# Two vision layers on one core: the step size moved into an exponential's bias, skips added to a diagonal, and shorter stage openings

## The chip, the cores and the metric

The kernel runs on one core of a Trainium2 chip. The metric is the device time of one execution in microseconds (us); lower is better. Five engines work side by side and are ordered only by semaphores: PE multiplies matrices (PEld is its loading of weights), DVE, ACT and POOL work elementwise, and SP issues the DMAs. Each engine takes its own instructions strictly in the order in which the program lists them.

## The reference

Two layers follow each other on 8 images of 64x64 tokens with 192 channels. Layer 0 is a state-space layer with 12 heads (two scan directions of 6 heads), a gate and an MLP. What matters of it:

```
dt = softplus(dt + dt_bias);  da = exp(dt * A);  dtx = dt[..., None] * xh
h = da_t * h + dtx_t * B_t;   y_t = sum_n h * C_t          # step by step over 4096 tokens
y = ys + Ds * xh
out = x + (y0 + y1) * silu(z) @ W_out;   out + W2(silu(W1 out + b1)) + b2
```

Layer 1 splits the channels: one half goes through three convolutions with batch norms, the other through a layer norm, a depthwise convolution and a selective scan in four directions with 192 channels and 16 states each; both halves are joined and the input added.

## The kernel before

**The main loop.** `selective_scan` computes the scan of layer 1. It runs over 3072 units, 384 per image. A unit is 8 channels with 16 states (128 partitions) and 1024 tokens. For each, SP fetches the step sizes (`fetch`, L1430), ACT makes the decays (`decay`, L1435, two units ahead), PE spreads the inputs (`spread`, L1443, one unit ahead), DVE weights them (L1458) and scans (L1465), POOL multiplies by C (L1467), ACT handles the last column (L1473, L1474), PE gathers four units at a time (L1485), ACT copies the result out of PSUM (y, L1490) and SP stores it. Every 16 units a tile is prepared (`prepare`, L1387 to L1430).

**Side stages.** While image b is scanned, the other work of later images runs beside it: for image b+1 `conv0`, `ssd` (layer 0's scan), `mlp0`, then for image b-1 `conv_branch` (with `scan_sums` aside) and `scan_outputs`, then `scan_inputs` and `transposed` for image b+1. Image 0 has its stages ahead of the loop, one after the other, and the last image's outputs come after it.

**Pacing.** Each unit has two halves, and in each `Beside.half` lets the current stage run on. Stages are generators: a number they yield is a cost that is taken from a credit, and the half ends when the credit is gone; an empty yield (`None`) ends the half at once, to let something land. `pause(n)` yields n of them. `spread_over` sets the credit per half so that the stages fill the image:

```
work = sum(self.costs.get(gen.__name__, 40.0) for gen in self.stages)
self.rate = own / halves + work / (halves - 13 * len(self.stages))
```

The costs are what the stages yielded for image 0 (190 and 78 for the branch and the outputs). Ahead of the loop, empty yields are passed over. `in_turn` interleaves the steps of one stage for successive items; `among` puts calls between the yields of a generator. All instructions are pinned to program order.

**The chunk scan.** `ssd` works through an image in 32 chunks of 128 tokens (for each direction two runs of 64 tokens). In each turn come `store`, `outputs`, `weigh`, `decays` and `fetch`, of successive chunks. `fetch` makes R on POOL (L594). `decays` loads X (L602, L605), transposes B and C (ps_t, copied by ACT to bc), and computes the exponents of the decays between all pairs of tokens for 6 heads x 64 columns in ps_d (L618, L619), from which ACT makes M by one exponential for each direction (L621, L624). `weigh` computes ps_g = B^T C (L634), scales the states (Hm, POOL, L637) and the inputs (xw, POOL, L639), multiplies M by ps_g (DVE, L643) and X by dt (dtx, POOL, L645). `outputs` adds to the states (ps_s, L655; Hm, DVE, L661; Hn, POOL, L663, and DVE, L677), multiplies them by C (ps_h, L671; yo, DVE, L681) and adds the pairs (ps_y): for each direction and head, M times dtx (L686), and for direction 0 also a diagonal `skip0` times X (L692), which holds Ds of both directions. `group` prepares dt and its running sums for 8 chunks at once (L533 to L577).

PSUM tiles outside the unit's own dB come from `cx.one`, which hands out four banks in rotation (eight ahead of the loop, while a second pool is open). A bank is free again when its last reader is done, so PE can wait for ACT or DVE to read what stood there.

Of the kernel before, what the change touches and what calls it, by code (L numbers as in the profile page):

```python
# [17 lines left out]
L = HH * WW  # L18
# [11 lines left out]
S = 64  # L30
# [79 lines left out]
def setup(cx, cp, dp, p0, p1):  # L110
# [105 lines left out]
    for n, v in (("eps", 1e-5), ("one", 1.0), ("minus", -1.0)):  # L216
        k[n] = cp.tile([128, 1], F32, tag=n, name=n)
        nc.gpsimd.memset(k[n], v)
# [77 lines left out]
def among(gen, calls):  # L296

    calls = list(calls)
    for n, cost in enumerate(gen):
        yield cost  # L300
        if n % 2 == 1 and calls:
            calls.pop(0)()
    for call in calls:
        call()
        yield None
# [72 lines left out]
def conv0(cx, x):  # L378
# [3 lines left out]
    with cx.pool("cw0") as wp, cx.pool("v0", 2) as vp:  # L382
# [98 lines left out]
        for j in range(NJ):  # L481
            pin(nc.sync.dma_start(out=diag[:, j], in_=k["diag0"][:, j]))
            yield None
        xp = wp.tile([128, 2 * NJ, 2 * NP0], F32, tag="xp0", name="xp0")
        for i in range(2):
            pin(nc.sync.dma_start(
                out=xp[64 * i : 64 * (i + 1)], in_=k["p0_xp"].rearrange("(j p) k m -> p j (k m)", p=64)
            ))
# [3 lines left out]
        yield from pause(2)  # L492
        load(1)
        yield from pause(2)
        load(1)
        for j in range(NJ):
            yield from project(0, j)
# [13 lines left out]
def ssd(cx):  # L511

# [14 lines left out]
    with cx.pool("g0", 2) as gp, cx.pool("s0", 2) as sp:  # L527
# [5 lines left out]
        def group(g):  # L533
# [19 lines left out]
            pin(nc.scalar.activation(dt, dt, AF.Softplus))  # L553
            cx.exp_again()
# [22 lines left out]
            groups[g] = both, over, *(t.rearrange(by_chunk, k=K2) for t in (dt, da, upto, toend))  # L577

        coming = group(0)
        for n in (8, 2, 2, 3, 2):  # L580
# [17 lines left out]
        def decays(c):  # L598
# [15 lines left out]
            M = sp.tile([128, 2, NH, S], F32, tag="M", name="M")  # L614
            R = st[c].pop("R")
            for d in range(2):
# [3 lines left out]
                if d == 1:  # L620
                    pin(nc.scalar.activation(flat(M[:, 0]), ahead, AF.Exp))  # L621
                yield 1.0
                ahead = ps
            pin(nc.scalar.activation(flat(M[:, 1]), ahead, AF.Exp))  # L624
            st[c].update(X=X, bc=bc, M=M)

        def weigh(c):

            _, over, dt, _, _, toend = groups[c // GC]
# [8 lines left out]
            xw = sp.tile([128, 2, NH, HP], F32, tag="xw", name="xw", bufs=1)  # L638
# [5 lines left out]
            dtx = sp.tile([128, 2, NH, HP], F32, tag="dtx", name="dtx", bufs=1)  # L644
            pin(nc.gpsimd.tensor_mul(dtx.rearrange(heads), X.rearrange(heads), bcast(dt[:, c % GC, :], 2, HP)))  # L645
            st[c].update(dtx=dtx, xw=xw, Hm=Hm)

        def outputs(c):

            both, over, _, _, upto, _ = groups[c // GC]  # L650
            X, bc, M, xw, dtx, Hm = (st[c].pop(v) for v in ("X", "bc", "M", "xw", "dtx", "Hm"))
# [1072 lines left out]
```

## Time and profile before

| | |
|---|---|
| median of 3 runs | 16537.61 us (16530.31 to 16537.72) |
| profiled execution | 16556.29 us, its span 16554.4 us |
| mean granted PE clock | 0.831 of full |
| DMA | 196 GB/s on average |
| first scan unit starts / last one starts | 913.1 us / 16290.4 us |

In the lines below, "L1465 DVE ... h<-dA,carry,dB 128x1024" is the instruction of line 1465 on DVE, the tiles that it writes and reads and their size, then how often it comes, its busy time in total, the mean duration of one in ns, and the idle time of the engine ahead of it with what ended that. A busy time counts overlapped instructions once, and a mean duration can overlap that of its neighbour. A window's line has its start and end, its length, and the busy time of each engine with the number of instructions.

### The profile page before, as it was taken

Reading aid. Unit: us, or ns where it says so; the run is one execution under the profiler, and the core shown is the slowest. Engines: PE = TensorE matmul, PEld = TensorE weight load, DVE = VectorE, ACT = ScalarE, POOL = GpSimd, SP = SyncE. Lnnn points to the kernel's source line nnn. Section 1 sums busy time; section 2 is a strip of 40 time slices with the busy share of each in tenths; the row PEclk is TensorE's granted clock in tenths of the full one; section 3 lists DMA queues with packets and bytes.
Section 4 is the critical chain, followed back from the end, with each engine's and each line's share of the span. In section 5 each row is a group of like instructions: output and inputs, shape, how many; then the busy total and the mean of one; then the engine's idle time right before and its main releaser. Section 6 shows DMA issues by size and latency. Waiting matters only on the chain.

```text
span 16554.4 us, 220424 instructions
## 1 busy us (share of the span) xinstructions
PE 13560.5 (82%) x75752; PEld 4803.7 (29%) x75752; DVE 12258.6 (74%) x9264; ACT 9901.5 (60%) x17354; POOL 10649.1 (64%) x5765
## 2 busy tenths in 40 slices
PE   8977887788977888888888789887898878878876
PEld 4423322332223321333213332233322333211111
DVE  2268888886778766887678876788767887778994
ACT  3365677565674656647566475665657556655653
POOL 3258766875568655686557865577655775566773
PEclk9987888889788896888878898788887889877766
DMA  3288878888787887888778878888778887788884
GB/s 90 84 218 198 214 196 227 194 209 202 182 226 192 202 208 184 222 193 207 205 195 208 199 199 207 206 202 198 196 195 212 200 209 203 193 224 201 214 209 125
DMA packets 1605044, 3248.22 MB, mean 196 GB/s; under 512 B 390536, under 2 KB 841752, under 8 KB 1603928
## 3 DMA queue, kind: packets, MB, share of 16 engines
q1 hardware_dynamic: 1603928, 3234.12, 78.5%
q8 instruction: 605, 9.91, 0.3%
q14 instruction: 511, 4.19, 0.1%
HBM read 2555.20 MB, written 678.18 MB: 195 GB/s over the span
## 4 chain that ended last, share of the span: by engine, by line
PE 41%; DMA 17%; DVE 16%; ACT 11%; POOL 8%; issue 5%; SPq 2%; DVEq 0%; POOLq 0%; ACTq 0%
DVE h L1465 9%; PE ps_cv L343 7%; DMA dA<-dld 5%; PE acc L1485 4%; DVE dB L1458 4%; PE ps_c L886 4%; POOL h L1467 3%; PE dB L1443 2%; ACT dA L1435 2%; PE ps_m L795 2%; PE ps_sum L1178 2%; PE ps_xp L1355 2%; DMA dus<-dud 2%; PE ps_y L686 1%; PE ps_var L1000 1%
## 5 line engine op out<-in xcount | busy, mean ns | idle before, releaser
L1467 POOL TENSOR_TENSOR h<-h,bc 128x1023 f32<-128x1023 f32 x3072 | 7229.2, 2354 | 4661.0 <-DVE h L1465 4123.4
L1465 DVE TENSOR_TENSOR_SCAN h<-dA,carry,dB 128x1024 f32<-128x1024 f32 x3072 | 7201.5, 2344 | 712.6 <-ACT dA L1435 224.1
L1458 DVE TENSOR_TENSOR dB<-dB,bc 128x1024 f32<-128x1024 f32 x3072 | 3742.3, 1218 | 1921.2 <-PE dB L1443 1909.4
L1435 ACT ACTIVATE dA<-dA,neg_a 128x1024 f32<-128x1024 f32 x3072 | 3505.9, 1141 | 44.2 <-DMA dA<-dld 39.1
L1485 PE MATMUL acc<-h,gather 128*32 128x512 f32 x12288 | 2310.3, 721 | 524.3 <-ACT h L1474 230.7
L1443 PE MATMUL dB<-dus,spread 24*128 24x512 bf16 x6144 | 1379.8, 434 | 849.4 <-DVE h L1465 764.0
L1490 ACT COPY y<-acc 128x512 f32<-128x512 f32 x1536 | 883.3, 575 | 944.0 <-PE acc L1485 818.5
L886 PE MATMUL ps_c<-p,conv_w 96*96 96x512 f32 x2304 | 1242.8, 668 | 70.2 <-ACT p L906 63.2
L1443 PEld LDWEIGHTS <-spread 24*128 24x128 bf16 x6144 | 309.6, 93 | 3099.6 <-issue 1452.3
L1473 ACT COPY carry<-h 128x1 f32<-128x1 f32 x3072 | 573.0, 187 | 947.5 <-DVE h L1465 944.4
L686 PE MATMUL ps_y<-dtx,M 64*64 64x64 f32 x12288 | 784.9, 258 | 333.6 <-DVE Hn L677 309.4
L1474 ACT ACTIVATE h<-h,bc 128x1 f32<-128x1 f32 x3072 | 905.2, 295 | 158.7 <-ACT carry L1473 3.0
L343 PE MATMUL ps_cv<-pad,diag 64*64 64x512 f32 x6912 | 835.6, 603 | 6.4 <-ACT y L1490 5.4
L686 PEld LDWEIGHTS ps_y<-dtx,M 64*64 64x64 f32 x12288 | 662.5, 169 | 492.7 <-issue 311.4
L1485 PEld LDWEIGHTS acc<-h,gather 128*32 128x32 f32 x12288 | 304.6, 117 | 1535.5 <-issue 938.2
L107 ACT ACT_TABLE_LOAD x577 | 740.3, 1283 | 10.2
L618 PE MATMUL ps_d<-R,after 128*128 128x384 f32 x1024 | 565.0, 642 | 72.5 <-POOL R L594 26.9
L613 ACT COPY bc<-ps_t 64x256 f32<-64x256 f32 x256 | 93.4, 365 | 855.9 <-PE ps_t L608 855.6
L886 PEld LDWEIGHTS ps_c<-p,conv_w 96*96 96x96 f32 x2304 | 368.5, 177 | 777.8 <-issue 686.8
L1355 PE MATMUL ps_xp<-u,xp 128*108 128x512 f32 x768 | 474.4, 706 | 98.9 <-DMA u<-u 86.1
L1394 POOL TENSOR_TENSOR du<-dl,u 128x1024 f32<-128x1024 f32 x192 | 452.2, 2355 | 127.0 <-ACT dl L1391 127.0
L373 PE MATMUL ps_h<-oa,w1a 128*128 128x256 f32 x1536 | 451.5, 414 | 58.6 <-ACT h L826 17.3
(243 smaller groups left out, 19239.9 us busy)
## 6 DMA issues: line engine op xcount, KB each, us to landing
dA<-dld SPq DMA_DIRECT2D x3072, 512.0 KB
dud<-terms SPq DMA_DIRECT2D x192, 768.0 KB
dus<-dud SPq DMA_DIRECT2D x2304, 64.0 KB
bc<-bcd SPq DMA_DIRECT2D x256, 512.0 KB
y<-yrows SPq DMA_DIRECT2D x256, 384.0 KB
u<-u SPq DMA_DIRECT2D x192, 512.0 KB
dld<-dl SPq DMA_DIRECT2D x192, 512.0 KB
y<-y SPq DMA_DIRECT2D x3072, 32.0 KB
```

What stands on the lines that cost most here:

```text
L343: pin(nc.tensor.matmul(ps[64 * b : 64 * (b + 1)].rearrange("p (h w) -> p h w", w=WW), lhsT=diag[:, t, :], rhs=pad[64 * i : 64 * (i + 1), b ...
L686: pin(nc.tensor.matmul(psy[d][here, h * HP : (h + 1) * HP], lhsT=M[here, d, h, :], rhs=dtx[here, d, h, :], start=True, stop=d == 1,))
L886: pin(nc.tensor.matmul(ps.rearrange("p (h w) -> p h w", w=WW), lhsT=w[:, t, :], rhs=pad[:, dy : dy + RB, dx : dx + WW], start=t == 0, stop ...
L1355: pin(nc.tensor.matmul(ps[:NXP], lhsT=k["xp"][:, g, t, :], rhs=u_of[m][t][:, here], start=t == 0, stop=t == 2))
L1435: pin(nc.scalar.activation(dAs[q], dAs[q], AF.Exp, scale=k["neg_a"][:, steps[m][1], t, i : i + 1]))
L1443: pin(nc.tensor.matmul(dBs[q][:, half, :], lhsT=k["spread"][at : at + 3 * UD, :], rhs=du_of[n][at : at + 3 * UD, i // 2, :], start=True, s ...
L1458: pin(nc.vector.tensor_mul(dBs[q], dBs[q], of(q)[0]))
L1465: pin(nc.vector.tensor_tensor_scan(order(h, g), order(dA, g), order(dB, g), carry, ALU.mult, ALU.add))
L1467: pin(nc.gpsimd.tensor_mul(h[:, rest], h[:, rest], C_[:, rest]))
L1474: pin(nc.scalar.activation(end, end, AF.Identity, scale=C_[:, last : last + 1]))
L1485: pin(nc.tensor.matmul(ps[32 * v : 32 * (v + 1)], lhsT=k["gather"], rhs=hs[q - 3 + v][:, here], start=True, stop=True))
L1490: pin(nc.scalar.copy(y[:, here], ps))
```

## The change

In `ssd`, the decays' exponent gets the logarithm of dt as a bias: exp(s + ln dt) = dt exp(s). The bias is a column for each head, so each of the two exponentials per chunk becomes six over 64 columns. Then M holds dt already, and dtx is not made; M is multiplied with X. `group` computes ln dt (with 1e-37 added) after softplus. The skips are added on POOL to direction 0's M, at the opening of `outputs`, and the skip matmuls are gone. xw gets two buffers. Yields of `outputs` fall from 1.7 and 1.1 to 1.1 and 1.1.

The openings of the stages are shortened: `conv0` loads its first diagonal alone and the others between the steps of the first projection (it had also loaded the second rows twice), `mlp0` begins its gate after three halves and loads the rest between its yields, `conv_branch` loads the second convolution's weights and `scan_inputs` its diagonals within the work; pauses in `ssd`, `transposed` and `scan_outputs` are shorter. `transposed` copies two parts between pauses, with four buffers. In `spread_over` 13 becomes 9.

```diff
-def among(gen, calls):
+def among(gen, calls, n=2):
...
-        if n % 2 == 1 and calls:
+        if i % n == n - 1 and calls:
             calls.pop(0)()
@@ conv0
-        for j in range(NJ):
+        def load_diag(j):
             pin(nc.sync.dma_start(out=diag[:, j], in_=k["diag0"][:, j]))
-            yield None
...
+        load_diag(0)
         yield from pause(2)
         for j in range(NJ):
             pin(nc.gpsimd.memset(pads[j], 0.0))
-        yield from pause(2)
+        yield from pause(1)
+        for j, calls in enumerate(([lambda: load_diag(1)], [lambda: load_diag(2)], [load_xp])):
+            yield from among(project(0, j), calls, 1)
         load(1)
-        yield from pause(2)
-        load(1)
-        for j in range(NJ):
-            yield from project(0, j)
@@ ssd, group
             pin(nc.scalar.activation(dt, dt, AF.Softplus))
+            ln_dt = gp.tile([128, GC * K2], F32, tag="ln_dt", name="ln_dt")
+            pin(nc.scalar.activation(ln_dt, dt, AF.Ln, bias=k["tiny"]))
             cx.exp_again()
@@ ssd
-        for n in (8, 2, 2, 3, 2):
+        for n in (7, 1, 1, 2, 1):
@@ ssd, decays
+            def exp(d, ps):
+                for h in range(NH):
+                    bias = groups[c // GC][2][:, c % GC, d * NH + h : d * NH + h + 1]
+                    pin(nc.scalar.activation(M[:, d, h, :], ps[:, h * S : (h + 1) * S], AF.Exp, bias=bias))
...
-                    pin(nc.scalar.activation(flat(M[:, 0]), ahead, AF.Exp))
+                    exp(0, ahead)
...
-            pin(nc.scalar.activation(flat(M[:, 1]), ahead, AF.Exp))
+            exp(1, ahead)
@@ ssd, weigh
-            xw = sp.tile([128, 2, NH, HP], F32, tag="xw", name="xw", bufs=1)
+            xw = sp.tile([128, 2, NH, HP], F32, tag="xw", name="xw")
...
-            dtx = sp.tile([128, 2, NH, HP], F32, tag="dtx", name="dtx", bufs=1)
-            pin(nc.gpsimd.tensor_mul(dtx.rearrange(heads), X.rearrange(heads), bcast(dt[:, c % GC, :], 2, HP)))
@@ ssd, outputs
+            pin(nc.gpsimd.tensor_add(M[:, 0], M[:, 0], k["skip0"]))
...
-                            psy[d][here, h * HP : (h + 1) * HP], lhsT=M[here, d, h, :], rhs=dtx[here, d, h, :],
-                            start=True, stop=d == 1,
+                            psy[d][here, h * HP : (h + 1) * HP], lhsT=M[here, d, h, :], rhs=X[here, d, h, :],
+                            start=True, stop=True,
                         ))
-                    if d == 0:
-                        for here in chunks:
-                            pin(nc.tensor.matmul(
-                                psy[d][here, h * HP : (h + 1) * HP], lhsT=k["skip0"][here, h, :], rhs=X[here, d, h, :],
-                                start=False, stop=True,
-                            ))
-                yield 1.7 - 0.6 * d
+                yield 1.1
@@ mlp0
-        for call in loads(0):
-            call()
-            yield None
-        pin(nc.sync.dma_start(out=w_out, in_=k["p0_w_out"].rearrange("(j p) m -> p j m", p=128)))
+        first, *calls = loads(0)
+        first()
...
+        calls.pop(0)()
         yield None
+        calls.pop(0)()
+        yield from pause(2)
+        yield from among(gate(0), calls + [load_out], 1)
+        yield None
+        add(0)
         yield from load_split(cx, w1, k["p0_w1"])
-        yield from gate(0)
-        add(0)
-        pin(nc.sync.dma_start(out=w2, in_=k["p0_w2"].rearrange("(f p) m -> p f m", p=128)))
         yield from turn(0)
-        yield from project(0)
-        for call in loads(1):
-            call()
-            yield None
+        yield from among(project(0), loads(1) + [load_2], 1)
@@ conv_branch
-        for n in ("conv1_w", "conv2_w"):
...
+        for r in range(3):
+            load_w(0, r)
+            yield None
...
+        yield from among(turns, [lambda r=r: load_w(1, r) for r in range(3)])
@@ scan_inputs
-            pin(nc.sync.dma_start(out=diag[n], in_=k["diag_" + n]))
-            yield from pause(2)
-        yield from pause(2)
+        yield from pause(4)
...
+        yield from among(turns, [
+            lambda n=n: pin(nc.sync.dma_start(out=diag[n], in_=k["diag_" + n])) for n in "ab"
+        ])
@@ transposed
-            yield from pause(1 if q < 3 else 3)
+            yield from pause(1 if q < 3 else 2)
...
-                part = tp.tile([whole.shape[0], L // 4], F32, tag="part", name="part", bufs=3)
+                part = tp.tile([whole.shape[0], L // 4], F32, tag="part", name="part", bufs=4)
...
-                yield 1.0
-                yield None
+                if q % 2 == 1:
+                    yield 1.0
+                    yield None
@@ scan_outputs
-                yield from pause(6)
+                yield from pause(4)
@@ spread_over
-        self.rate = own / halves + work / (halves - 13 * len(self.stages))
+        self.rate = own / halves + work / (halves - 9 * len(self.stages))
```

## The prediction

> **What bounds the kernel now.** I read the page's busy shares first, then the chain that ended last.
>
> ```profile
> PE 13560.5 (82%) x75752; PEld 4803.7 (29%) x75752; DVE 12258.6 (74%) x9264; ACT 9901.5 (60%) x17354; POOL 10649.1 (64%) x5765
> PE 41%; DMA 17%; DVE 16%; ACT 11%; POOL 8%; issue 5%; SPq 2%; DVEq 0%; POOLq 0%; ACTq 0%
> ```
>
> No engine is full and the chain goes through all of them, so the average decides nothing. The scan loop (913 to 16,300 us) has 3072 units, and each needs a scan (2344 ns) and a weighing (1218 ns) on DVE, 3.56 us. In the timeline, units without side work start at 6932.58, 6936.18, 6939.79 and 6943.39: 3.60 us. That is the floor. A middle image has 384 units in 2010 us; 384 x 3.60 is 1382 us, and the other 630 us are what the side stages add. I therefore cut the image that begins near 6624 us into its stages (columns: length, busy time of PE, PEld, DVE, ACT, POOL, granted clock, DMA share, GB/s). The first line is the chunk scan of image 0, ahead of the loop.
>
> ```profile
> 173.00:479.00 306.00, 277.48 (x3848) 157.82 (x3846) 128.83 (x256) 82.85 (x171) 194.45 (x173) 0.96 0.40 105
> ...
> 6926.00:7000.00 74.00, 46.97 (x326) 19.44 (x318) 54.90 (x46) 40.60 (x76) 55.95 (x34) 0.66 0.86 174
> 7000.00:7469.00 469.00, 374.26 (x3674) 177.16 (x3674) 396.19 (x403) 221.12 (x426) 398.80 (x252) 0.80 0.80 191
> 7474.00:7906.00 432.00, 364.59 (x1664) 153.51 (x1664) 332.06 (x237) 316.13 (x528) 268.66 (x121) 0.91 0.81 204
> 7908.00:8215.00 307.00, 278.09 (x770) 76.77 (x766) 195.15 (x110) 144.34 (x264) 168.85 (x93) 0.93 0.84 216
> ...
> 8569.00:8616.00 47.00, 15.91 (x47) 2.13 (x46) 25.64 (x16) 32.58 (x40) 23.75 (x11) 0.57 0.85 239
> ```
>
> In the chunk scan (7000 to 7469) DVE and POOL are busy for 84 and 85%, ACT for 47%. A chunk takes 15.8 us there, DVE idle for some 2.4 us of it. In the conv branch (7908) PE is at 91% and sets the pace. In the opening of the chunk scan (6926) PE has little to do. In image 0's chunk scan PE is at 91%, with a chunk every 7.26 us from 250 us on.
>
> **The skip matmuls.** The groups, each shape apart:
>
> ```profile
> L692 PE MATMUL ps_y<-X,skip 64*64 64x64 f32 x6144 | 485.4, 255 | 0.0
> ...
> L645 POOL TENSOR_TENSOR dtx<-X,dt 128x768 f32<-128x768 f32 x256 | 376.2, 1469 | 0.0
> ...
> L946 POOL TENSOR_TENSOR o<-o,sh 96x512 f32<-96x512 f32 x64 | 81.3, 1270 | 42.5 <-ACT carry L1473 42.5
> ...
> L624 ACT ACTIVATE M<-ps_d 128x384 f32<-128x384 f32 x256 | 125.4, 490 | 149.7 <-PE ps_d L619 149.5
> ...
> L922 ACT ACTIVATE p<-ps_c,bn_b,bn_g 96x64 f32<-96x64 f32 x56 | 21.8, 388 | 0.0
> ```
>
> 6144 instructions over 256 chunks are 24 per chunk. Their 255 ns overlap; what they occupy is the distance of starts. Two timelines show it, at half and at full clock:
>
> ```profile
> 7202.45 0.45 PE L692 MATMUL ps_y<-X,skip 64*64 64x64 f32 x4
> 7202.88 0.45 PE L692 MATMUL ps_y<-X,skip 64*64 64x64 f32 x4
> ```
>
> ```profile
> 7271.88 0.28 PE L692 MATMUL ps_y<-X,skip 64*64 64x64 f32 x4
> 7272.12 0.28 PE L692 MATMUL ps_y<-X,skip 64*64 64x64 f32 x4
> ```
>
> Between two lines lie eight instructions (four of L686): 0.43 us or 0.24 us, so 54 or 30 ns each, 1.3 or 0.7 us for 24. In image 0 the chunk's first set, skips included, lasts 1.61 us, half of it 0.8. PE is last there, so 0.75 x 32 = **24 us** go.
>
> In the loop less arrives, for what follows on PE waits anyway. The waits of 7040 to 7440 us (26 chunks; total, times, longest):
>
> ```profile
> PE ps_y L686 <- DVE Hn L677: 33.8, 18, 3.9
> ...
> DVE Hn L677 <- POOL Hn L663: 18.1, 13, 2.9
> ...
> DVE Hm L661 <- PE ps_s L655: 17.0, 10, 3.8
> ...
> PE ps_s L655 <- POOL xw L639: 8.7, 8, 1.8
> ...
> PE ps_h L671 <- ACT y L1490: 5.0, 6, 1.2
> ```
>
> The second direction's matmuls wait for DVE's Hn in 18 of 26 chunks; without skips they just wait longer. Taking in each chunk the time from the end of Hn to the start of that second set, but no more than half of the first set, I get 0.57 us per chunk that PE can gain, of about 1.05 removed. DVE, the fullest beside POOL, profits from about half: -0.3.
>
> **POOL.** dtx (1469 ns) goes; the addition of skip0 on 128x384 comes, by L946 1270 x 384/512 = 0.95 us. Net -0.52 per chunk. It stands behind R and waits for DVE's weighting of M from an earlier half; behind it on POOL are Hn and the unit's own product h, for which Hn's addition on DVE and the gather on PE wait. DVE waits 18.1/26 = 0.7 us per chunk for POOL's Hn and PE 0.33 for xw, so I take -0.3. Giving xw a second buffer removes no wait that I see.
>
> **ACT.** Two exponentials of 384 columns become twelve of 64 with a bias column. L922 has 64 columns with scale and bias columns, 388 ns; the same pair on 512 columns costs 776 and bias alone (L940) 680, so a scale column is 96 and ours should be 292. Neighbours overlap:
>
> ```profile
> 7202.25 0.29 ACT L1474 ACTIVATE h<-h,bc 128x1 f32<-128x1 f32 x1
> ...
> 7202.45 1.13 ACT L1435 ACTIVATE dA<-dA,neg_a 128x1024 f32<-128x1024 f32 x1
> ```
>
> 0.29 us long, 0.20 apart. So 12 x 0.20 = 2.4 against 2 x 0.40 = 0.8: **+1.6 us per chunk**. The Trainium skill ("ScalarE: Activation LUTs", What ACT_TABLE_LOAD costs) speaks harder against the change: about 280 ns plus 0.833 per column with a bias column, less 93 of overlap, hence 240 each, and 2.9 - 0.8 = +2.1. With its figure the loop's sum below would be 22 us worse, if the same fifth of it counts; I keep the row. What queues behind the burst on ACT is a decay (needed two units later, some 10 us), and the copy y, which frees a PSUM bank that PE already waits for (5.0 us above, and 3.0 at ps_g). The burst also keeps its own two banks longer; ps_h starts in the median 2.1 us after the last exponential. I charge a fifth, +0.3; bounds 0 and +1.6. The logarithm comes once in eight chunks: an ACTIVATE of 0.3 and at most one more table load of 1283 ns, 0.2 us per chunk on an engine half idle: nothing, and 45 us if it were all exposed.
>
> Per loop chunk -0.3 - 0.3 + 0.3 = -0.3; seven images, 224 chunks: **-67 us**. Bounds per chunk -1.2 (PE and POOL pass whole) to +1.3 (the burst passes whole, less half of PE's gain).
>
> **The clock.** Granted clock is 0.80 here, and 0.66 in the opening where PE idles. The Trainium skill ("TensorE: Matmul & The Clock Gate", Part 1) says half rate is the default, and only a stretch of some 3.4 us of activity lifts it: taking matmuls away can slow those that stay. By the row nothing is lost; by the rule, at 0.75, the 315 us of PE left in the stage become 21 us more, 147 over seven images if all showed. PE idles 20% here, so I take nothing and leave it to the upper end.
>
> **The openings and the rate.** Halves that carry no side work, by counting the empty yields at the openings: before 12 + 17 + 15 + 7 + 6 + 6 + 14 = 77 in the seven stages, after 6 + 12 + 8 + 4 + 4 + 4 + 9 = 47. So 15 units more carry work. The rate is 450/768 + work/(768 - 13 x 7), work being 1164 by the yields: 2.305 per half. After: work 1141 (19 less for skips, 4 less in transposed) over 768 - 9 x 7: 2.204. The same end is reached by going slower. Where PE sets the pace, a unit more gives 3.60 less its own PE work (L1443, L1485, L1355, L1387: 4495/3072 = 1.46), 2.1 us. PE does so in about 0.55 of them: 15 x 0.55 x 2.1 = -17 us per image; where DVE does, nothing.
>
> Against it, the first work now comes sooner after its loads: conv0's 4 halves after its image rows instead of 10, mlp0's 3 after x instead of 8, branch 4 instead of 7. A half is 1.8 us, and X here took 6 to 8 us to land. PE takes its work in order, so a late weight holds the next dB, and DVE after it. POOL's first addition in mlp0 waits for rows that were asked for only three halves earlier, and h waits behind it. I estimate 2 to 4 us in each of five stages, +15. SP gets fewer loads in one go at conv0 (one duplicate load of rows goes), and transposed, where ACT waits for whole, ends a few units earlier, which helps the next image's u: -5. Together -7 per image, seven times: **-49 us** (bounds -150 and +100).
>
> **Sum.** -24 - 67 - 49 = -140. The profiled execution took 16,556.3 us (span 16,554.4 plus 1.9), the median of the runs is 16,537.6, 0.11% less. 16,556 - 140 = 16,416, as a median **16,400 us**. The tail after 16,300 has no skips and no pacing: unchanged.
>
> **Rivals.** (1) Slower: ACT's burst. In the chunk scan y and the bank of the second exponential come late, PE stands still with dB behind, and DVE loses it. At +1.0 per chunk: 224 x 1.0 = 224, less 24 and 49: 16,690. It decides from +0.33 per chunk. For it: PE already waits for y in some 13 of 26 chunks. Against: ACT is half idle, and DVE uses ps_h only 2.6 us or more after it starts. (2) Nothing to measure: DMA landing sets the openings, so the stalls grow by what the pauses lose, and the chunk is bound by DVE whatever goes: -24 alone, 16,515. For it: DMA is at 80 to 95%. (3) Much faster: POOL and PE relief pass whole, 224 x -1.2 = -269, openings -17 x 7 = -119, with -24: -412, 16,125. For it: DVE's idle 2.4 us per chunk are waits for just these. Against: 0.57 is all that PE gains.
>
> **How the numbers follow.** My forecast 0.50 (own range 16,310 to 16,470), rival 1 0.22, rival 2 0.14, rival 3 0.14. A difference under 0.2% can't be told from none. Faster 0.50 + 0.14 = 0.64, same 0.14, slower 0.22. The range leaves out half of rivals 1 and 3 at the ends: 16,200 to 16,640.
>
> **What would show it.** Right: L692 gone; chunk scan stage about 10 us shorter per image, image 0's by 24; waits of PE for DVE Hn longer; twelve exponentials at about 290 ns; the empty stretch at 6926 shorter, and clock in the branch unchanged. Wrong: new large waits of PE for ACT M or y (rival 1), of PE or POOL for weights and rows at the openings (rival 2), or a granted clock in the chunk scan well under 0.80.

## The result, and the profile after

The changed kernel takes 16,422.68 us (median of 4 runs, 16,421.88 to 16,438.50); the kernel before took 16,533.96 us beside it (16,500.32 to 16,537.72). The ratio is **0.9939, with a 95% interval of 0.9922 to 0.9957**, so 0.6% faster (the medians lie 111 us apart). 16,400 was forecast. The total came out nearly as worked out; most of its terms did not, as the experiments show.

The page's busy shares and the chain that ended last, of the kernel after:

```profile
PE 13372.1 (81%) x69608; PEld 4636.5 (28%) x69608; DVE 12230.0 (74%) x9264; ACT 10412.7 (63%) x20023; POOL 10527.5 (64%) x5766
PE 30%; DMA 16%; DVE 14%; ACT 13%; POOL 7%; issue 5%; SPq 2%; DVEq 0%; ACTq 0%; POOLq 0%
```

The 6144 skip matmuls are gone, and PE is busy for only 188 us less; ACT is busy for 511 us more, POOL for 122 us less. The chain still goes through all the engines.

The middle image that begins at 6552 us, cut where each stage issues its first instruction (columns as before: length, busy time of PE, PEld, DVE, ACT, POOL, granted clock, DMA share, GB/s). These are the chunk scan, `mlp0`, the conv branch, `scan_outputs` and `scan_inputs`:

```profile
6870.00:7404.00 534.00, 400.06 (x3214) 171.92 (x3208) 439.45 (x441) 305.70 (x807) 428.51 (x282) 0.74 0.76 186
7404.00:7852.00 448.00, 375.79 (x1679) 157.01 (x1676) 338.68 (x241) 331.50 (x546) 273.87 (x124) 0.90 0.79 200
7852.00:8157.00 305.00, 282.87 (x771) 77.62 (x768) 195.14 (x111) 144.37 (x265) 170.61 (x94) 0.93 0.85 219
8157.00:8306.00 149.00, 127.36 (x285) 28.12 (x288) 109.27 (x90) 116.61 (x183) 91.71 (x48) 0.71 0.72 172
8306.00:8483.00 177.00, 163.65 (x780) 39.86 (x774) 158.15 (x103) 140.04 (x236) 118.53 (x62) 0.91 0.88 222
```

The last two stages in the kernel before, which the prediction did not look into:

```profile
8215.00:8373.00 158.00, 135.45 (x271) 29.34 (x270) 104.96 (x87) 114.35 (x178) 90.53 (x47) 0.67 0.68 162
8373.00:8574.00 201.00, 188.99 (x782) 43.94 (x782) 159.75 (x102) 140.48 (x235) 117.96 (x61) 0.76 0.77 194
```

`scan_inputs` went from 201 to 177 us with the same number of PE instructions, at a granted clock of 0.91 instead of 0.76. Its matmuls were not touched by the change. The chunk scan, where the arithmetic changed, went from 548 to 534 us, but with five units fewer in it, and its clock fell from 0.78 to 0.74.

Stages carry different numbers of units before and after, so lengths mislead. From the starts of DVE's scans in the timeline I counted the units of each stage and took 3.60 us for each from its length. What remains, the **excess**, is what the stage adds to the loop. The table has its means over the five middle images, in us per image, for all kernels of this study (the last four columns: mean granted clock in the chunk scan and in `scan_inputs`, start of the first scan, ratio to the kernel before):

| kernel | conv0 | chunk scan | mlp0 | branch | outputs | inputs | transposed | sum | clock, chunk scan | clock, inputs | first scan | ratio |
|---|---|---|---|---|---|---|---|---|---|---|---|---|
| before | 47.5 | 200.9 | 123.1 | 109.1 | 71.5 | 50.2 | 22.8 | 625 | 0.80 | 0.76 | 913 | 1 |
| after | 51.2 | 197.2 | 131.4 | 112.0 | 61.5 | 24.5 | 24.8 | 603 | 0.75 | 0.89 | 902 | 0.9939 |
| arithmetic only | 51.0 | 205.1 | 121.6 | 109.0 | 72.6 | 47.7 | 22.5 | 630 | 0.72 | 0.77 | 905 | 1.0010 |
| openings only | 61.9 | 207.4 | 126.9 | 113.1 | 55.5 | 37.1 | 34.0 | 636 | 0.77 | 0.82 | 915 | 1.0066 |
| openings only, paced as after | 54.7 | 205.9 | 130.6 | 112.1 | 66.0 | 20.4 | 26.3 | 616 | 0.79 | 0.92 | 911 | 0.9997 |
| after, inputs opened as before | 51.6 | 198.4 | 132.1 | 110.2 | 59.1 | 44.0 | 25.2 | 621 | 0.75 | 0.79 | 909 | 1.0021 |
| before, inputs' opening only | 51.0 | 198.3 | 120.0 | 110.5 | 66.6 | 36.2 | 24.1 | 607 | 0.79 | 0.89 | 916 | 0.9962 |
| before, matmuls added in inputs | 51.2 | 196.5 | 122.7 | 108.6 | 65.1 | 37.7 | 17.4 | 599 | 0.80 | 0.90 | 934 | 0.9960 |
| after, one exponential | 52.3 | 190.4 | 132.2 | 110.9 | 59.8 | 24.3 | 25.9 | 596 | 0.73 | 0.89 | 904 | 0.9922 |
| after, exponentials twice | 53.4 | 270.5 | 130.1 | 109.2 | 61.4 | 27.5 | 24.4 | 677 | 0.70 | 0.87 | 939 | 1.0264 |
| after, skips by matmul | 52.6 | 185.5 | 130.8 | 110.9 | 59.7 | 28.9 | 24.2 | 593 | 0.81 | 0.87 | 916 | 0.9916 |
| after, no skips | 52.4 | 185.9 | 129.4 | 109.8 | 57.7 | 27.3 | 25.8 | 588 | 0.75 | 0.88 | 897 | 0.9882 |
| after, skips by matmul, ln dt by matmul | 53.1 | 191.1 | 134.6 | 115.3 | 64.3 | 24.7 | 25.5 | 609 | 0.84 | 0.88 | 945 | 0.9961 |
| after, skips by matmul, matmuls added in outputs | 54.5 | 184.4 | 131.2 | 109.2 | 54.6 | 28.5 | 24.5 | 587 | 0.81 | 0.86 | 914 | 0.9886 |

How far can a row be trusted? Each is one profiled execution, while the ratio is from medians; the profile of "ln dt by matmul" was the slowest of its twelve executions (58 us above their median), that of "matmuls added in inputs" the fastest of its ten (44 below). And from image to image of one kernel a stage's excess scatters by 1 to 8 us (standard deviation). So a difference of less than some 5 us between two rows of a stage says little.

From before to after, `scan_inputs` gives 25.7 us per image and `scan_outputs` 10; the chunk scan, where half of the forecast gain was to be, gives 3.7, which is within that scatter, and `mlp0`, conv0 and the branch take 15 back. The profiled spans differ by 117.7 us: 11 until the first scan, 109 in the five middle images, while the rest of the loop and the tail lost 2.

The groups that answer to those of before:

```profile
L696 PE MATMUL ps_y<-X,M 64*64 64x64 f32 x12288 | 605.6, 270 | 418.6 <-issue 232.7 <-DVE Hn L687 93.5 <-POOL M L661 74.1
L661 POOL TENSOR_TENSOR M<-M,skip 128x384 f32<-128x384 f32 x256 | 254.8, 995 | 0.1
L624 ACT ACTIVATE M<-ps_d,ln_dt 128x64 f32<-128x64 f32 x3072 | 669.1, 335 | 314.6 <-PE ps_d L630 304.6 <-POOL h L1482 2.7 <-POOL xw L650 2.7
```

POOL's addition of the skips takes 995 ns, as estimated, and it is a new releaser of PE's ps_y. One exponential takes 335 ns. The waits of 400 us of a chunk scan of the kernel after, 6960 to 7360 us (total, times, longest):

```profile
DVE Hm L671 <- PE ps_s L665: 25.3, 19, 3.5
...
DVE Hn L687 <- POOL Hn L673: 18.3, 15, 2.4
...
PE ps_y L696 <- DVE Hn L687: 11.5, 7, 3.1
...
PE ps_s L665 <- POOL xw L650: 7.5, 8, 1.9
...
PE ps_y L696 <- POOL M L661: 5.7, 5, 1.5
```

Before, PE waited 33.8 us for DVE's Hn here, and the forecast said that this wait would grow when the skips went. It shrank to 11.5; which part of the change did that, the experiments separate below. POOL's Hn is waited for as long as before (18.1 then), and M from POOL is new.

### The profile page after: what moved, and what is told of

Its sections match the earlier page's. It is cut to its first block, busy times and chain, and to the rows that moved or that the text cites. A ratio compares the mean times of both kernels' runs of the same rounds, so it can differ in the third digit from the quotient of the medians.

```text
span 16436.7 us, 210821 instructions
## 1 busy us (share of the span) xinstructions
PE 13372.1 (81%) x69608; PEld 4636.5 (28%) x69608; DVE 12230.0 (74%) x9264; ACT 10412.7 (63%) x20023; POOL 10527.5 (64%) x5766
## 4 chain that ended last, share of the span: by engine, by line
PE 30%; DMA 16%; DVE 14%; ACT 13%; POOL 7%; issue 5%; SPq 2%; DVEq 0%; ACTq 0%; POOLq 0%
DVE h L1480 9%; DMA dA<-dld 5%; PE acc L1500 5%; DVE dB L1473 4%; PE ps_c L895 4%; PE ps_cv L343 3%; POOL h L1482 3%; ACT dA L1450 3%; PE dB L1458 2%; DMA dus<-dud 2%; PE ps_sum L1193 1%; ACT L107 1%; PE ps_m L799 1%; PE ps_y L696 1%; ACT h L830 1%
## 5 line engine op out<-in xcount | busy, mean ns | idle before, releaser
L1450 ACT ACTIVATE dA<-dA,neg_a 128x1024 f32<-128x1024 f32 x3072 | 3512.9, 1144 | 29.3 <-DMA dA<-dld 24.1
L1500 PE MATMUL acc<-h,gather 128*32 128x512 f32 x12288 | 2364.1, 730 | 596.5 <-ACT h L1489 329.0
L895 PE MATMUL ps_c<-p,conv_w 96*96 96x512 f32 x2304 | 1287.7, 685 | 37.9 <-ACT p L915 26.9
L696 PE MATMUL ps_y<-X,M 64*64 64x64 f32 x12288 | 605.6, 270 | 418.6 <-issue 232.7
L624 ACT ACTIVATE M<-ps_d,ln_dt 128x64 f32<-128x64 f32 x3072 | 669.1, 335 | 314.6 <-PE ps_d L630 304.6
L343 PE MATMUL ps_cv<-pad,diag 64*64 64x512 f32 x6912 | 841.0, 605 | 7.1 <-ACT y L1505 5.1
L696 PEld LDWEIGHTS ps_y<-X,M 64*64 64x64 f32 x12288 | 548.8, 180 | 606.5 <-issue 275.5
L629 PE MATMUL ps_d<-R,after 128*128 128x384 f32 x1024 | 606.4, 685 | 31.2 <-ACT bc L618 14.6
```

The costliest lines, as they stand in the source:

```text
L343: pin(nc.tensor.matmul(ps[64 * b : 64 * (b + 1)].rearrange("p (h w) -> p h w", w=WW), lhsT=diag[:, t, :], rhs=pad[64 * i : 64 * (i + 1), b ...
L696: pin(nc.tensor.matmul(psy[d][here, h * HP : (h + 1) * HP], lhsT=M[here, d, h, :], rhs=X[here, d, h, :], start=True, stop=True,))
L895: pin(nc.tensor.matmul(ps.rearrange("p (h w) -> p h w", w=WW), lhsT=w[:, t, :], rhs=pad[:, dy : dy + RB, dx : dx + WW], start=t == 0, stop ...
L1450: pin(nc.scalar.activation(dAs[q], dAs[q], AF.Exp, scale=k["neg_a"][:, steps[m][1], t, i : i + 1]))
L1500: pin(nc.tensor.matmul(ps[32 * v : 32 * (v + 1)], lhsT=k["gather"], rhs=hs[q - 3 + v][:, here], start=True, stop=True))
```

## The experiments

**Halves of the change.** First the chunk scan's arithmetic alone, with the stages opened and paced as before:

```diff
 # kernel after
-self.rate = own / halves + work / (halves - 9 * len(self.stages))
+self.rate = own / halves + work / (halves - 13 * len(self.stages))
 # and conv0, mlp0, conv_branch, scan_inputs, transposed, scan_outputs, group(0) open as before,
 # outputs yields 1.7 and 1.1 as before
```

> The kernel before with the chunk scan's arithmetic changed alone (ln dt as bias, twelve exponentials, no dtx, skips added on POOL, two xw buffers); all openings, all yields and the rate as before. Forecast's sum: image 0 gives 24 us and 224 loop chunks 0.3 us each, together 91 us, ratio 0.9945. Clock theory (the two traces show the gain where scan_inputs runs, where the granted clock rose from 0.77 to 0.91, and next to none in the chunk scan): the arithmetic gives the 11 us of image 0 and about 4 us per image, 40 us, ratio 0.9976, and scan_inputs keeps its clock of 0.77. ACT rival: slower, 1.003 or more.

Measured: 16,545.12 us, ratio 1.0010 (0.9994 to 1.0026). Then the openings and the new rate alone, with the arithmetic of before:

```diff
 # kernel before
-self.rate = own / halves + work / (halves - 13 * len(self.stages))
+self.rate = own / halves + work / (halves - 9 * len(self.stages))
 # and all openings as after
```

> The kernel before with the shorter openings and the rate (9 for 13) alone; the chunk scan's arithmetic and yields as before. Forecast's sum: 49 us, ratio 0.997, spread over all stages. Clock theory: scan_inputs alone gives some 25 us per image at a granted clock over 0.9, the other stages nothing or a few us back: 70 to 110 us, ratio 0.994 to 0.996. If DMA landing sets the openings: 1.000.

Measured: 16,628.52 us, ratio 1.0066 (1.0040 to 1.0092). Neither half gains; together they give 0.9939. The sum of my terms assumed that they add. In the chunk scan of the kernel with the arithmetic only the clock is 0.72, against 0.80 before, and the excess is 205.1 against 200.9, the same within the scatter.

**Pacing.** In the kernel with the openings only the rate was 2.231 per half, not after's 2.204, because its chunk scan still reports 1.7 for a first direction with skips. One number changed brings the same pacing as after:

```diff
 # kernel with the openings only
-                yield 1.7 - 0.6 * d
+                yield 1.1
```

> The kernel with the openings alone, with one number changed: the cost that the chunk scan tells the planner for its first direction is 1.1 as after instead of 1.7, so that the rate is 2.204 per half as in the kernel after instead of 2.231 (the arithmetic is that of before). If the pacing, so the place at which each stage meets the units of the loop, is what made the openings alone slower: conv0's excess falls from 62 to 51-55, that of transposed from 34 to 25, that of scan_inputs from 37 to 25-30, ratio 0.994 to 0.999. If the new arithmetic itself is needed: ratio stays 1.004 to 1.009.

Measured: 16,510.41 us, ratio 0.9997 (0.9982 to 1.0011). The stages did as the pacing theory said (conv0 54.7, transposed 26.3, `scan_inputs` 20.4), the total came out just above its bracket. A planner's constant, with no instruction added or removed, is worth 0.7% here. It sets the pace of all stages, and how much of the chunk scan runs in a half; what of this gave the gain was not separated. On this pacing the arithmetic does gain: 0.9939 / 0.9997 is 0.6%, some 95 us, and the chunk scan's excess falls by 8.7 us per image. On the pacing of before the same arithmetic gained nothing there. Why, I did not find.

**Which opening.** The kernel after, with only the opening of `scan_inputs` undone:

```diff
 # kernel after, scan_inputs
+            pin(nc.sync.dma_start(out=diag[n], in_=k["diag_" + n]))
+            yield from pause(2)
-        yield from pause(4)
+        yield from pause(2)
-        yield from among(turns, [lambda n=n: ... for n in "ab"])
+        yield from turns
```

> The changed kernel with the opening of scan_inputs alone as before (both diagonals loaded ahead, six empty halves). Forecast's sum: two empty halves more per image, about 10 us in all, ratio 0.9945. Clock theory, if it is this stage's own opening that keeps the clock up: its 25 us per image are lost, about 170 us, ratio 1.004, with the clock in the stage back at 0.77. Clock theory, if it is the rate and the distance of its pieces: no change against the changed kernel, ratio 0.994, clock over 0.9.

Measured: 16,548.10 us, ratio 1.0021 (1.0007 to 1.0035). All the other stages stay as after; `scan_inputs` goes from 24.5 to 44.0, at a clock of 0.79. In the combination this one opening carries the whole gain. And it alone, in the kernel before (the reverse of that diff):

> The kernel before with one part of the change: scan_inputs loads its two sets of depthwise weights (diag_a, diag_b) during the first two row blocks instead of ahead of a pause, four empty half-units instead of six. If that part alone holds the gain of the openings: the stage's excess falls from 50 us to about 25, clock there 0.88, total 16,526 - 7 x 20 = 16,390, ratio 0.992 (the kernel after with this part undone lost 0.8%). If the gain needs the other parts (the phase in which the stage meets the loop): ratio 0.998 to 1.004, clock in the stage 0.8 or less.

Measured: 16,451.65 us, ratio 0.9962 (0.9947 to 0.9977), excess 36.2, clock 0.89. So it gains by itself, about two thirds of what the whole change gives.

**Is it the clock?** A low clock can be a mere consequence of waiting. If it is what makes the stage slow, PE work added to raise it should make the stage faster:

```diff
 # kernel before, scan_inputs, convolve, ahead of depthwise
+            for i in range(12):
+                pin(nc.tensor.matmul(
+                    pss[0][:, : NH * S], lhsT=k["ident16"], rhs=k["hide"].rearrange("p h c -> p (h c)"), start=True, stop=True
+                ))
```

> The kernel before, with twelve matmuls of 128x128 by 384 columns (bf16) put ahead of each of the eight depthwise convolutions of scan_inputs; what they write is overwritten, so they only add work: 8 x 12 x 160 ns = 15 us of PE per image at full clock. Theory A, the granted clock of this stage is what the new opening of scan_inputs gains: the clock in the stage rises from 0.76 to 0.9 or more, and the stage's excess over 3.60 us per unit falls from 50 us by 10 or more in spite of the added work; the total falls by 70 to 150 us. Theory B, the clock there is a consequence of PE's waits and costs nothing: the stage becomes 10 to 20 us longer, the total 100 us more (ratio 1.006).

Measured: 16,469.16 us, ratio 0.9960 (0.9945 to 0.9976). The row of `scan_inputs` in this kernel:

```profile
8330.00:8517.00 187.00, 175.70 (x865) 48.83 (x866) 156.34 (x100) 136.44 (x231) 115.36 (x60) 0.90 0.81 209
```

With 83 PE instructions more than before, PE is busy for 13 us less (188.99 then), the stage is 14 us shorter, and the excess is 37.7 instead of 50.2, with nearly the same number of units (41.0 and 42.4). What was added carries nothing that is used and loads only PE, so the low clock costs time here and is no mere consequence; the total gained 59 us, a little less than the forecast's 70. (Adding work also shifts the stage against the units; a shift of the same length without PE work was not run.) Where PE stays in the low clock is in before's timeline, PE alone, and in a cut of the same stretch by clock:

```profile
8439.64 1.10 PE L980 MATMUL ps_mean<-xt,m 96*96 96x512 f32 x2
8442.93 0.39 PE L1443 MATMUL dB<-dus,spread 24*128 24x512 bf16 x2 [2.19 <-DVE h L1465]
8443.25 9.16 PE L343 MATMUL ps_cv<-pb,diagb 64*64 64x512 f32 x22
...
8491.79 7.09 PE L343 MATMUL ps_cv<-pb,diagb 64*64 64x512 f32 x16 [1.39 <-DVE xt L1007]
```

```profile
8434.00:8440.00 6.00, 5.85 (x27) 1.27 (x26) 5.87 (x4) 5.61 (x9) 4.75 (x3) 1.00 1.02 286
8444.00:8472.00 28.00, 28.00 (x66) 5.73 (x62) 17.23 (x13) 14.96 (x28) 13.17 (x8) 0.50 0.73 182
8475.00:8488.00 13.00, 13.00 (x90) 3.08 (x82) 12.47 (x8) 9.23 (x16) 8.69 (x4) 1.00 0.75 170
8493.00:8519.00 26.00, 26.00 (x62) 4.85 (x58) 14.59 (x9) 15.04 (x24) 12.04 (x7) 0.50 0.61 174
8524.00:8544.00 20.00, 20.00 (x124) 4.72 (x118) 18.36 (x11) 14.66 (x25) 16.30 (x10) 1.00 0.78 206
```

PE stands for 2.19 us, the clock drops to half, and it stays there for 28 us in which PE is busy without a gap. The same once more from 8493 us, after a gap of 1.39 us. Both times the convolution of the second channel group (pb, L343) follows the gap. In the kernel after, a convolution of the second group runs at full clock, with 16 matmuls in 3.65 us instead of 7.09; PE stands later, and the first group's convolution (pa) follows:

```profile
8372.43 3.65 PE L343 MATMUL ps_cv<-pb,diagb 64*64 64x512 f32 x16
...
8389.79 0.39 PE L1458 MATMUL dB<-dus,spread 24*128 24x512 bf16 x2 [1.73 <-DVE h L1480]
8390.11 1.31 PE L343 MATMUL ps_cv<-pa,diaga 64*64 64x512 f32 x8
```

```profile
8391.00:8394.00 3.00, 3.00 (x20) 1.04 (x16) 3.00 (x3) 2.12 (x5) 1.18 (x1) 0.50 1.03 151
8396.00:8476.00 80.00, 78.18 (x442) 19.00 (x434) 72.66 (x44) 67.01 (x108) 54.86 (x28) 1.00 0.85 207
```

Here half rate lasts some 3 us, and the next 80 us run at full clock. The opening moved the stage against the units, so that the gaps fell elsewhere. With the matmuls added, the second of those two convolutions of before, in the same image:

```profile
8440.56 4.00 PE L1062 MATMUL ps_cv<-hide,ident 128*128 128x384 bf16 x12 [0.77 <-DVE xt L1007]
8444.48 4.22 PE L343 MATMUL ps_cv<-pb,diagb 64*64 64x512 f32 x16
```

There is a gap here too, and the added twelve take 4.00 us at half clock; from 8445.67 us on, soon after the convolution's start, the clock is full for 68 us. The 16 matmuls take 4.22 us instead of 7.09.

**The skips.** The kernel after with the skips as matmuls again, the rest unchanged:

```diff
-            pin(nc.gpsimd.tensor_add(M[:, 0], M[:, 0], k["skip0"]))
...
+                    if d == 0:
+                        for here in chunks:
+                            pin(nc.tensor.matmul(psy[d][here, ...], lhsT=k["skip0"][here, h, :], rhs=X[here, d, h, :], start=False, stop=True))
```

> The kernel after, but with the skips by 24 matmuls per chunk as before and no addition of skip0 on POOL; all else, dt in the exponential's bias and the pacing too, stays. By the prediction (PE relief 0.3 us per chunk, and POOL loses 0.95 us of work per chunk that the addition cost): between -0.1 and +0.3 us per chunk, +0 to +70 us. By the clock's rule (matmuls keep the clock up, so their removal gained nothing in the loop): granted clock in the chunk scan back from 0.75 to 0.80, image 0 about 11 us longer, loop within 30 us of the kernel after.

Measured: 16,378.03 us, ratio 0.9916 (0.9899 to 0.9934): 0.23% better than the kernel after. The intervals of the two overlap; their executions do not (16,367 to 16,391 us, and 16,422 to 16,439). Then without skips in either form (the term D x is left out of the result): the first line of that diff alone.

> The kernel after without the addition of skip0 on POOL, and with no matmuls in its place: the term D x of the chunk scan is left out of the result. With the skips as matmuls the excess of the chunk scan over 3.60 us per unit was 185.5 us per image at a granted clock of 0.81, with the addition 197.2 at 0.75. Theory P, POOL's addition (0.95 us per chunk in the chain M, addition, ps_y) is the price: without it the excess falls to 185 or less, though the clock stays at 0.75 or below; ratio to the kernel before 0.990 to 0.992. Theory C, the clock that falls with the removed matmuls is the price: the excess stays at 193 to 200, ratio 0.993 to 0.995.

Measured: 16,319.44 us, ratio 0.9882 (0.9863 to 0.9902). The chunk scan's row of the two kernels, with matmuls and without:

```profile
6877.00:7391.00 514.00, 396.69 (x3982) 187.99 (x3976) 439.29 (x442) 304.57 (x807) 399.50 (x250) 0.82 0.80 193
```

```profile
6862.00:7379.00 517.00, 393.31 (x3211) 166.32 (x3208) 438.01 (x441) 304.64 (x806) 397.84 (x250) 0.75 0.80 192
```

771 matmuls fewer, and PE is busy for 3.4 us less: the clock went from 0.82 to 0.75, and those that stay are slower. The excess is the same, 185.5 and 185.9, and so is PE's wait for DVE's Hn, 9.1 and 9.0 us in 400: it is not the removed skips that changed it. In the chunk scan of the loop the removal is worth nothing. (The whole kernel gained 59 us: 19 until the first scan; most of the other 40 lies outside the chunk scan, 1 to 2 us per image in a stage, and is not explained.) Between no skips and POOL's addition lie 11.3 us per image, 0.35 us per chunk: the addition stands between DVE's weighting of M and ps_y, and ahead of Hn on POOL. In image 0 it is otherwise: its chunk scan's last instruction starts at 479.6 us with skip matmuls, at 463.1 without, and at 467.9 with the addition. There PE is the bound, and the matmuls cost 16.5 us.

**ACT's burst.** The kernel after with one exponential per direction (the step sizes of five of six heads are left out of M, so the result is another one):

```diff
-                for h in range(NH):
-                    bias = groups[c // GC][2][:, c % GC, d * NH + h : d * NH + h + 1]
-                    pin(nc.scalar.activation(M[:, d, h, :], ps[:, h * S : (h + 1) * S], AF.Exp, bias=bias))
+                bias = groups[c // GC][2][:, c % GC, d * NH : d * NH + 1]
+                pin(nc.scalar.activation(flat(M[:, d]), ps, AF.Exp, bias=bias))
```

> The changed kernel with one exponential of 384 columns per direction instead of six of 64: all heads get the bias of the first head of their direction, so dt of the other heads is left out of M. It takes away ACT's burst alone (about 1.6 us of ACT per chunk). Forecast's sum: the burst costs 0.3 us per chunk, so 67 us faster than the changed kernel, ratio 0.990. If ACT's burst is hidden whole: ratio 0.994. If the burst is what kept the chunk scan from gaining: 0.984 or less, and waits of PE for ACT go with it.

Measured: 16,395.86 us, ratio 0.9922 (0.9903 to 0.9941): 27 us less than after, a difference that the two intervals do not separate, or 0.12 us per chunk; in the chunk scan's excess it is 6.8 us per image, 0.21 us per chunk. In the other direction, every exponential twice:

```diff
-                    pin(nc.scalar.activation(M[:, d, h, :], ps[:, h * S : (h + 1) * S], AF.Exp, bias=bias))
+                    for again in range(2):
+                        pin(nc.scalar.activation(M[:, d, h, :], ps[:, h * S : (h + 1) * S], AF.Exp, bias=bias))
```

> The kernel after with each of the twelve exponentials per chunk issued twice (same result): ACT +12 x 0.24 = 2.9 us per chunk. If ACT has slack at this place, as the run with one exponential per direction showed for the first 1.6 us (27 us in all, 0.12 per chunk): 0.2 to 0.5 us per chunk, +50 to +110 us, ratio 1.003 to 1.007. If the slack is used up by then (rival 1's mechanism past its threshold): half or more passes, +1.5 us per chunk or more, +330 us, ratio 1.02.

Measured: 16,937.89 us, ratio 1.0264 (1.0238 to 1.0290). Its chunk scan, its exponentials, and the product of H and C on PE:

```profile
7132.00:7735.00 603.00, 438.66 (x3208) 183.69 (x3208) 439.78 (x441) 421.92 (x1189) 427.07 (x281) 0.70 0.69 165
```

```profile
L625 ACT ACTIVATE M<-ps_d,ln_dt 128x64 f32<-128x64 f32 x6144 | 1620.5, 310 | 371.4 <-PE ps_d L631 257.9 <-POOL Hm L649 10.0 <-POOL xw L651 2.8
L682 PE MATMUL ps_h<-Hn,bc 32*64 32x384 f32 x992 | 432.6, 653 | 272.7 <-ACT M L625 217.6 <-DVE Hn L688 39.7 <-DVE Hm L672 13.7
```

Against after, ACT has 1620.5 - 669.1 = 951 us more over 256 chunks, 3.7 each; the excess grew by 73.3 us, 2.3 per chunk. The first 1.6 us of the burst pass by an eighth, the next 3.7 by six tenths. PE's ps_h now waits 217.6 us for M, as the bank that it takes in turn is still being read by the exponentials. That is rival 1, mechanism and place; the change stopped short of it.

**A better version?** The burst can be avoided by adding ln dt in PSUM, in two bf16 parts, on top of the kernel with skip matmuls:

```diff
-                pin(nc.tensor.matmul(ps, lhsT=k["ident16"], rhs=flat(k["hide"]), start=False, stop=True))
+                pin(nc.tensor.matmul(ps, lhsT=k["ident16"], rhs=flat(k["hide"]), start=False, stop=False))
+                for part in (2, 6):     # ln dt rounded to bf16, and what is left of it
+                    ln = groups[c // GC][part][:, c % GC, d * NH : (d + 1) * NH]
+                    pin(nc.tensor.matmul(ps.rearrange(...), lhsT=k["ident16"], rhs=bcast(ln, 2, S), start=False, stop=part == 6))
```

> The kernel after with the skips as matmuls and with ln dt added in PSUM: split into two bf16 parts, each spread over 64 columns per head by a matmul with the unit matrix (four matmuls of 128x384 more per chunk, 0.64 us of PE at full clock), so that one exponential of 384 columns per direction is enough. A possible better version than both. If ACT's burst costs the 0.12 us per chunk that the run with one exponential showed, and the added matmuls lift the clock rather than delay: 16,378 - 27 = 16,350, ratio 0.990, clock in the chunk scan 0.83 or more. If PE's added work is on the path there: +0.64 us x 224 = up to +140 us, less 27: ratio up to 0.998.

Measured: 16,443.76 us, ratio 0.9961 (0.9947 to 0.9975), worse than with the burst (0.9916): image 0, bound by PE, starts its first scan at 945 us instead of 916. In its slowest execution, which was the profiled one, the chunk scan's excess is 191.1 instead of 185.5, although the clock is 0.84.

Last, the finding on the clock in the stage with the lowest one that still has much PE work, `scan_outputs`, again on the kernel with skip matmuls:

```diff
                 ps = cx.one("ps_z")[:size]
+                for i in range(12 if n == "a" else 0):
+                    pin(nc.tensor.matmul(ps[:, : NH * S], lhsT=k["ident16"], rhs=..., start=True, stop=True))
```

> The kernel after with the skips as matmuls (ratio 0.9916 by itself), and with twelve matmuls of 128x128 by 384 columns added ahead of the gate's matmul of each of the eight row blocks of scan_outputs, where the granted clock was 0.72 and the excess 60 us per image; what they write is overwritten. If it goes as in scan_inputs: clock there 0.85 or more, excess 50 or less in spite of 15 us more work, ratio 0.986 to 0.989. If the low clock there comes from PE's idle stretches (12 us for the rows of y) and costs nothing: excess 65 to 75, ratio 0.994 to 0.998.

Measured: 16,321.73 us, ratio **0.9886** (0.9867 to 0.9905), the best of the kernels that compute everything. The stage's row:

```profile
8147.00:8288.00 141.00, 122.75 (x381) 34.66 (x384) 108.91 (x90) 115.83 (x183) 91.51 (x48) 0.86 0.77 181
```

Clock 0.87 instead of 0.72 on the mean, excess 54.6 instead of 59.7: half of what was hoped for in the stage, and no more than the scatter. The total fell by 0.3%, with intervals that just overlap and executions that do not (16,302 to 16,366 us, and 16,367 to 16,391). So 96 matmuls of no use at least cost nothing.

## Why the total was right and its terms were not

**Image 0, forecast -24: -11.** The mechanism held. The size did not: "0.75 x 32" took every chunk as bound by PE, and 16.5 us passed. The addition that came for it takes 5 back, which I had charged nothing in image 0.

**PE's relief in the loop, forecast -0.3 per chunk: nothing.** The step that failed is "PE idles 20% here, so I take nothing" for the clock. The rule that I set aside for the row of 0.80 (the Trainium skill, "TensorE: Matmul & The Clock Gate", Part 1) was the right one: the clock fell to the 0.75 that it was costed with, and removal and slower rest cancelled: PE busy 396.69 and 393.31 us. PE's wait for Hn did not grow either.

**POOL, forecast -0.3 net: about -0.5.** On equal pacing, going from openings only to skips by matmul takes the product dt x away, gives xw its second buffer and brings the burst: 205.9 - 185.5 = 20.4 us per image, 0.64 per chunk. With the burst's 0.21 that is 0.85 for the product and the buffer, and 0.35 come back with the addition. This supposes that the parts add. The path that I had named, POOL's Hn behind this work and DVE waiting for it, is there. DVE's waits in the whole trace, with the old arithmetic on after's pacing, with the skips by matmul, without skips, and with the addition:

```profile
DVE Hn L679 <- POOL Hn L665: 251.4, 151, 6.4
DVE Hn L686 <- POOL Hn L672: 91.1, 57, 7.1
DVE Hn L686 <- POOL Hn L672: 94.6, 61, 8.6
DVE Hn L687 <- POOL Hn L673: 229.5, 153, 8.1
```

With it PE's wait for DVE's Hn fell from 367.1 to 62.1 us. The 995 ns addition brings back most of the wait that the 1469 ns product had caused, and PE waits for M besides (74.1 us), where it waited little for the product (16.3 on that pacing). I had priced the two by the difference of their durations.

**ACT's burst, forecast +0.3: +0.21.** The duration was wrong, 292 ns by the row against 335 measured; the skill's figure ("ScalarE: Activation LUTs", What ACT_TABLE_LOAD costs: 280 ns and 0.833 per column, 333 for 64) was right. The burst's length was right nevertheless: 669.1 - 250.8 = 418 us of busy time, 1.63 us per chunk, since neighbours overlap more than the page's 93 ns would have it. The fifth that I let pass was an eighth.

So on the pacing of after the chunk's terms are 0, -0.5 and +0.21. Their sum, -0.29, is no check: they come from the same rows of the table as the whole, 205.9 - 197.2 = 8.7 us, -0.27 per chunk. The forecast was -0.3: errors of +0.3, -0.2 and -0.1 cancelled, which is luck. On the pacing of before the same arithmetic gained nothing.

**The openings, forecast -49.** On after's pacing, -5 by themselves (0.9997, with an interval of -30 to +18 us); on their own pacing +109. The two terms, 17 us for spread units and 15 for stalls, missed what mattered. The stalls are there, and of at least the size that was put on them: conv0, `mlp0` and the branch together lost 15 us per image, with whatever the spread units gave them. In conv0 (before and after, the stage's waits):

```profile
DVE dB L1458 <- PE dB L1443: 38.4, 31, 8.1
```

```profile
DVE dB L1473 <- PE dB L1458: 48.9, 15, 19.2
```

The unit's dB now waits up to 19.2 us instead of 8.1. It stands in PE's queue behind conv0's projection, which waits for the image's rows (the timeline of PE, kernel after):

```profile
6573.08 3.75 PE L373 MATMUL ps_in<-xa,w_ina 128*128 128x512 f32 x4 [7.27 <-DMA xa<-in_x_dram]
```

That is the stall that the prediction named, and PE comes out of it at half clock (3.75 us for the group; 1.98 for the next such at 6580 us). But before, PE stood in this opening too, for 6.61 us until the inputs of a unit (dus) had landed, and came out as slowly (3.78 us); what is added is 10.5 us of waits for dB in this image, and 3.7 us of excess on the mean. What paid for it is the clock in `scan_inputs`, 25.7 us per image, which appears in no term of mine. I cut the middle image into stages and quoted the chunk scan and the branch; the two stages that I left out show 0.76 and 0.67 with PE busy for 94 and 86% (the rows at the top). That was the sign: busy and slow. That the total came within 23 us of the forecast is therefore in good part luck.

**Of the rivals:** much faster (3) needed PE's relief to pass, and there was none. Nothing to measure (2) describes openings and arithmetic when each is alone. ACT's burst (1) is real, as the doubled exponentials show; at its true size it stood at 0.21 per chunk, under the 0.33 from which it was to decide.

## What to carry to other kernels

Before costing a removed matmul, look for the stages in which PE is busy and its granted clock is low: there PE's time depends also on what it did just before, and taking work away can be worth nothing, adding it can gain. A wait that moves by a few microseconds (an opening, a planner's constant) shifted this loop by 0.4 to 0.8%, as much as its arithmetic did; so measure the parts of a change together and apart, and do not add their effects. An operation moved to another engine is priced by the chain in which it stands there, not by its duration.

## What the runs showed of the hardware that I had not expected

Half clock can outlast a short gap by far: after PE had stood for 2.19 us it ran for 28 us at 0.50 with PE busy all the time, and after 1.39 us for another 26. It needs no gap at all. In the kernel before, with mostly the second group's convolution on PE:

```profile
8563.25:8566.67 3.42, 3.42 (x18) 0.92 (x16) 3.33 (x2) 1.23 (x2) 2.01 (x2) 1.00 1.06 281
8566.67:8570.10 3.43, 3.20 (x11) 0.38 (x8) 3.30 (x3) 3.29 (x6) 2.17 (x2) 0.50 1.03 248
```

PE is busy for all 3.42 us, and the clock falls; all five middle images have this fall. Of the 521 falls between 920 and 16,200 us of that kernel, only 28 came after PE had stood for nearly the whole of the 3.41 us before; the median is 1.9 us.

The Trainium skill ("TensorE: Matmul & The Clock Gate", Part 1) has the clock fall after an idle window of some 3.4 us and rise about 4 us into sustained activity. The rise is what the gap at 8388 us of the kernel after shows (some 3 us), and the added matmuls (4.00 us of them ran at half clock); the falls after less idle time and the long spells are not what it says, and the measurement decides.

The long spells began with the depthwise convolution of the second group, whose matmuls use 64 rows of the array at a time, the short one with that of the first group, which keep all 128 rows busy by turns. This repeats. In the convolutions of `scan_inputs`, over the traces of all fourteen kernels, the 76 spells at half clock of 20 us or more all hold 26 to 36 matmuls of the second group; the 62 spells with matmuls of the first group and none of the second end within 6.8 us; and with the 128x128 matmuls added ahead of each convolution no spell is longer than 6.8 us. That matmuls on part of the array do not lift the clock fits all of this. It was not tested by itself, with nothing but the rows changed.
